# Mixture-of-experts macaron layer: the search for the other experts' thresholds in two goes of four experts instead of three goes of two, its sums shared by VectorE transposes, the residual copied inside DRAM, the rows' factors in halves

## The chip, the cores and the metric

The kernel runs on one core of a Trainium2 chip. The metric is the device time of one execution in microseconds (us). Three runs of the kernel before the change took 1978.52, 1975.33 and 1978.26, a median of 1978.26. The core has five engines, each with its own queue of instructions that it works through in order: PE (TensorE, the matrix products, with PEld for its weight loads), DVE (VectorE), ACT (ScalarE), POOL (GpSimd) and SP (which here only starts transfers). Transfers run on 16 DMA engines.

## The reference

The input `x` holds 4 x 2048 = 8192 tokens of 256 numbers. Three updates follow one another, each with a layer norm before it:

```python
x = x + 0.5 * ffn(layernorm(x), router_w, wg, wu, wd)
x = x + attention(layernorm(x), ...)
x = x + 0.5 * ffn(layernorm(x), router_w, wg, wu, wd)
```

`ffn` is a mixture of 8 experts. Each token goes to the two with the largest router probabilities, with weights that sum to one. An expert takes at most `capacity = int(1.25 * 8192 / 8) = 1280` tokens, those with the largest weights; where weights are equal, the earlier token comes first.

```python
order = jnp.lexsort((-fw, fe))                 # by expert, then by falling weight
rank = jnp.arange(N * K) - starts[se]
keep = rank < capacity
...
eo = jnp.einsum('ecf,efd->ecd', silu(g) * u, wd)   # g = disp @ wg, u = disp @ wu, F = 1024
out = zeros.at[st].add(gathered * (sw * keep)[:, None])
```

So for each expert one has to know the weight of the 1280th token (a threshold, and how many of the tokens that equal it still fit). A threshold is a 32-bit number, and finding it is the "search" below.

## The kernel before

The order in time is: the first router and `route()` (to about 92 us), the experts of the first feed-forward layer (to about 890), the attention (to about 1125), `route()` again, the experts of the second layer, and the last scatters.

**Routing.** `first_router` (L1522) loads x, computes mean and variance of every token on VectorE (L1565), and the logits on PE with router weights `wrx`, from which VectorE has taken the mean (L1609); `wrx` is first cleared by POOL (L1598). `choose` (L280) turns logits into weights. Its inner `for_rows` (L372) makes four factors per token and expert that are appended to each token's row, and `write_rows` (L387) sends the rows to DRAM (`rows`), from where the experts gather their tokens.

**The search.** Class `Pair` (L393) finds the thresholds of two experts at once. Each expert's weights lie on 64 partitions, in 4 copies (`COPIES`). A round tests 4 candidates per expert. In the first pair's rounds, counting is on VectorE and all of `route()` waits for it. For the other six experts, `Others` (L524) holds three pairs and gives out their work one step at a time by `others.step()`. In `Pair.steps()` (L427) a round is: ScalarE's `sign` (L432) compares 512 numbers on each partition with that partition's candidate `mark` and sums the signs; PE's `reach` (L436) adds the sums over partitions; VectorE (L437, L440) counts the candidates that are below the threshold and moves `mark`. There are 7 rounds on the upper 16 bits and 7 on the lower ones, then steps that mark (L469 ff., `tail` L491) the tokens above the threshold and equal to it, place them by two scans (L391, L507 to L514), transpose back on PE (L517) and write `slot_lo`: 24 steps for each pair. The first pair takes expert 0 and 1.

**Where the steps stand.** `route()` (L537) takes a step in its rounds 0, 3 and 4 and in every even round from 6, and one in its tail. `first_list` and `first_turn` (L819) take some. In the expert stage, `aside(k)` (L1040) is called at places in the written order of chunk k's work, and takes one step every time until nothing is left.

**The experts.** A layer has 16 chunks of 640 rows, two per expert. `units(k)` (L888) forms the gate and up products by a scheme like Strassen's, in four parts p = 0 to 3, with three PSUM banks in turn (`banks`, L884). In each part, products are named by their number: after the fifth product there is a call to `aside` in the odd chunks, after the fourth one in all chunks for p = 0 to 2; `down(k)` (L1093) forms the down product and calls `aside` once near its end. Within the experts, PE, VectorE and ScalarE work in the order in which the code names the operations, so an operation that waits holds up all that follows it on its engine; POOL's order is a scheduler's. POOL also issues the gathers of rows (L775) and the scatters of results into `dst` (L1048), which adds to what is there.

**The residual.** In the first layer, the results are added to `acc`, a DRAM copy of x. It is written from SBUF (`xw`) by four transfers of 2 MB on SP's queue (L1622), three ahead of the rows, and one behind them. Expert 0's down weights (`wdt`, L720, `load_down`) follow, and expert 1's weights once gather 0 has been issued and has finished (`after`).

**Set-up.** Constants are made in lines 88 to 215, most of them on POOL, whose queue holds them in the order of a scheduler ahead of the clearing of `wrx`.

## Time and profile before

The profile is of one execution that took 1976.69 us.

| what | us |
|---|---|
| three runs, median | 1978.26 (1975.33 to 1978.52) |
| the profiled execution | 1976.69 |
| its span, first to last instruction | 1974.9 |
| PE busy | 1866.0 (94%) |
| VectorE busy | 1372.7 (70%) |
| ScalarE busy | 1030.4 (52%) |
| POOL busy | 1030.3 (52%) |
| first issue of gather 0 in layer 1 | 84.33 |
| first result `y` of layer 1 | 134.9 |
| first scatter into `acc` | 146.1 |

A row of a timeline gives start, duration, engine, line, operation, output and inputs with partitions x elements, and in brackets how long the engine was idle before it and whose end it waited for. In the windows, a row gives the stretch, its length, the busy time and number of instructions of PE, PEld, VectorE, ScalarE and POOL, the mean granted clock of PE (1 is full), and what share of the DMA engines was busy. In the rows of the 40 slices, each digit stands for 49.4 us of the span, in tenths.

### The profile page before, as it was taken

What the parts mean: (1) busy time and instruction counts of PE and PEld (TensorE: products, weight loads), DVE (VectorE), ACT (ScalarE), POOL (GpSimd) and SP (SyncE); (2) the same over time, 40 slices, a digit from 0 to 9 for tenths busy, and PEclk for the clock granted to TensorE, in tenths of its full rate; (3) what the DMA queues carried; (4) which work ended last, traced back from release to release, by engine and by line L of the source; (5) the groups of instructions that cost most, each with busy time, mean ns of one, the idle gap of its engine ahead of it and who ended that gap; (6) DMA issues with size and microseconds to landing.
All of it is one profiled execution on the core that took longest, in us unless ns stands there. A gap on an engine that the chain in (4) does not pass through costs nothing.

```text
span 1974.9 us, 26091 instructions
## 1 busy us (share of the span) xinstructions
PE 1866.0 (94%) x8882; PEld 1338.4 (68%) x8882; DVE 1372.7 (70%) x2677; ACT 1030.4 (52%) x2598; POOL 1030.3 (52%) x1061
## 2 busy tenths in 40 slices
PE   7499999999999999999999659999999999999997
PEld 5366766676667777776888536666666666777776
DVE  8678677776777676646677667867686767676763
ACT  5273747374736463325566437374737473737332
POOL 6434555555555555535555435555545554555552
PEclk9599999999999999999999869999999999999999
DMA  9912232222222221115012541313131313132121
GB/s 346 308 50 75 46 74 47 71 50 71 50 71 50 71 50 28 29 22 178 22 43 90 201 160 18 92 25 96 22 90 26 95 26 88 30 96 28 31 28 19
DMA packets 108005, 148.90 MB, mean 75 GB/s; under 512 B 7512, under 2 KB 94560, under 8 KB 107872
## 3 DMA queue, kind: packets, MB, share of 16 engines
q1 hardware_dynamic: 76992, 103.16, 15.3%
q0 software_dynamic: 30720, 43.93, 13.7%
q8 instruction: 70, 1.15, 0.2%
q14 instruction: 63, 0.52, 0.1%
q10 hardware_dynamic: 160, 0.14, 0.1%
HBM read 91.11 MB, written 56.10 MB: 75 GB/s over the span
## 4 chain that ended last, share of the span: by engine, by line
PE 46%; DVE 4%; ACT 2%; issue 1%; POOL 1%; DMA 1%; POOLq 0%; SPq 0%; DVEq 0%; ACTq 0%
PE mm L899 23%; PE mm L1114 11%; PE py L1412 3%; PE pc L1354 3%; PE qp L1295 3%; DVE ct L840 1%; PE back L1066 1%; PE tr L801 1%; PE trq L1342 1%; DVE junk_a L562 1%; PE trx L1287 1%; DVE key L514 0%; PE ix L699 0%; ACT lo L693 0%; POOL out_dram L1048 0%
## 5 line engine op out<-in xcount | busy, mean ns | idle before, releaser
L899 PE MATMUL mm<-xs,ws 128*128 128x320 f32 x1536 | 479.3, 435 | 1.7 <-DVE u L840 1.7
L843 POOL TENSOR_TENSOR ct<-ct 128x320 f32<-128x320 f32 x360 | 337.0, 936 | 200.9 <-DVE ct L930 151.7
L899 PEld LDWEIGHTS mm<-xs,ws 128*128 128x128 f32 x1536 | 282.2, 190 | 116.8 <-DVE ct L840 6.6
L840 DVE TENSOR_TENSOR ct<-u,mm 128x640 f32<-128x640 f32 x256 | 209.5, 819 | 151.3 <-PE mm L899 110.5
L775 POOL DMA_INDIRECT r<-rows,ixs x160 | 156.6, 979 | 273.3 <-ACT eo L1047 197.1
L927 ACT ACTIVATE ct<-ct 128x960 f32<-128x960 f32 (+1 forms) x192 | 141.2, 735 | 299.2 <-DVE ct L840 285.9
L840 DVE TENSOR_TENSOR ct<-ct,mm 128x640 f32<-128x640 f32 x288 | 236.0, 819 | 72.9 <-PE mm L899 57.2
L1114 PE MATMUL mm<-ct,wds 128*128 128x320 f32 x960 | 279.6, 433 | 1.0 <-DVE ct L840 1.0
L693 ACT ACTIVATE lo<-from_below,behind_lo 128x129 f16<-128x129 f16 x896 | 272.8, 395 | 0.0
L1114 PEld LDWEIGHTS mm<-ct,wds 128*128 128x128 f32 x960 | 178.7, 190 | 75.0 <-DVE ct L840 7.0
L1114 PE MATMUL mm<-ct,wdt 128*128 128x320 f32 x720 | 217.2, 438 | 0.0
L1048 POOL DMA_INDIRECT acc<-eo,ixs x80 | 128.0, 1600 | 146.4 <-ACT eo L1047 128.4
L1048 POOL DMA_INDIRECT out_dram<-eo,ixs x80 | 127.9, 1599 | 146.3 <-ACT eo L1047 128.4
L899 PE MATMUL mm<-xsT,wgt 128*128 128x320 f32 x512 | 189.9, 453 | 3.0 <-ACT p L939 2.0
L899 PE MATMUL mm<-xsT,wut 128*128 128x320 f32 x512 | 179.6, 432 | 0.0
L930 DVE TENSOR_TENSOR ct<-ct 128x640 f32<-128x640 f32 (+1 forms) x128 | 158.1, 1235 | 22.0 <-ACT ct L927 22.0
L1114 PEld LDWEIGHTS mm<-ct,wdt 128*128 128x128 f32 x720 | 133.4, 193 | 49.3 <-issue 4.2
L840 DVE TENSOR_TENSOR u<-p,mm 128x640 f32<-128x640 f32 x126 | 103.4, 821 | 87.6 <-PE mm L899 56.1
L899 PE MATMUL mm<-xsT,ws 128*128 128x320 f32 x512 | 161.8, 439 | 2.4 <-DVE ct L840 2.4
L939 ACT COPY p<-mm 128x640 f32<-128x640 f32 x126 | 86.4, 686 | 90.1 <-PE mm L899 74.5
L899 PEld LDWEIGHTS mm<-xsT,ws 128*128 128x128 f32 x512 | 97.4, 191 | 43.9 <-DVE ct L840 4.3
L899 PEld LDWEIGHTS mm<-xsT,wut 128*128 128x128 f32 x512 | 97.3, 190 | 40.6 <-issue 0.2
(340 smaller groups left out, 2932.9 us busy)
## 6 DMA issues: line engine op xcount, KB each, us to landing
wgt<-in_L_ffn_wg_dram SPq DMA_DIRECT2D x16, 1024.0 KB
wut<-in_L_ffn_wu_dram SPq DMA_DIRECT2D x16, 1024.0 KB
wdt<-in_L_ffn_wd_dram SPq DMA_DIRECT2D x16, 1024.0 KB
rows<-xw SPq DMA_DIRECT2D x6, 2240.0 KB
xw<-in_L_attn_x_dram SPq DMA_DIRECT2D x16, 512.0 KB
acc<-xw SPq DMA_DIRECT2D x4, 2048.0 KB
out_dram<-xw SPq DMA_DIRECT2D x16, 512.0 KB
xw<-acc SPq DMA_DIRECT2D x15, 512.0 KB
```

The source lines that it names most:

```text
L693: nc.scalar.activation(lo[:, t, :], from_below, AF.Sign, bias=at, scale=1.0)
L775: gathers[k].append(nc.gpsimd.indirect_dma_start(out=r, out_offset=None, in_=src[:, :], in_offset=bass.IndirectOffsetOnAxis(ap=lists[e][:, ...
L840: nc.vector.tensor_tensor(o, a, b, op)
L843: nc.gpsimd.tensor_tensor(o, a, b, op)
L899: nc.tensor.matmul(ps, a, b, start=start, stop=True, skip_group_check=not start)
L927: nc.scalar.activation(h(p)[:, qs, :], h(p)[:, qs, :], AF.Silu)
L930: engine.tensor_tensor(h(p)[:, qs, :], h(p)[:, qs, :], hT(p)[:, qs, :], ALU.mult)
L939: nc.scalar.copy(p1, ps)
L1048: ins = nc.gpsimd.indirect_dma_start(out=dst[:, :], out_offset=bass.IndirectOffsetOnAxis(ap=lists[e][:, i0 + i : i0 + i + 1], axis=0), in_ ...
L1114: nc.tensor.matmul(ps, a(p), b(p), start=(p == 0 and not more), stop=(p == NF - 1), skip_group_check=more)
L1295: nc.tensor.matmul(qp[i][:, k, 0:W1], xT[i][:, k, c, :], wqx[:, c, :], start=(c == 0), stop=(c == DC - 1))
L1354: nc.tensor.matmul(pcs[b][:, c, 0 : D + 1], eks[i][:, k, c * P : (c + 1) * P], ring[i % 4][:, k, :], start=(first and k == 0), stop=(last ...
```

## The change

1. The other six experts are searched by class `Quad` in two goes of four experts with 32 partitions each and 2 copies. The first takes experts 2 to 5, the second experts 4 to 7, of which it keeps 6 and 7. With 2 candidates instead of 4, there are 9 + 11 rounds instead of 7 + 7, and 28 steps to a go. `marked`, `placed` and `back` work on 256 columns instead of 128, and what was two steps is one (`placed`).
2. In the expert stage (`far`), the sums over partitions of a round are made on VectorE: a transpose of 32 x 32 blocks of the sums into 32 columns of `shift` (read as half floats) and a reduction into two columns of `rstd`. In `route()`, two PE products do it.
3. The steps have places and due times: `step_at` takes a step only if the place's time (49 us for each chunk, plus the place's own) has reached the time when the last step was taken plus its stated length (7.5 us for a round, 3.2 in chunk 1). The fifth product is followed by a place in all chunks, and for p = 3 too.
4. `route()` takes steps in odd rounds from 5 (five instead of four) and two in its tail instead of one; `first_turn` takes four instead of three.
5. `acc` is filled by four transfers from x to `acc` inside DRAM, behind gather 0 and ahead of expert 1's weights on SP. Expert 0's down weights are loaded with its others.
6. In the first routing, the rows' factors are made in two halves of the tokens; the copy `raw` comes between them.
7. The set-up constants change accordingly (a ladder for 2 copies, `quad_of`, `quad_ahead`, `portions`, `flip`, `quads`), and some are gone.

```diff
-    minus_half_of = const.tile([P, P], F16, name="minus_half_of")
-    nc.gpsimd.tensor_scalar(minus_half_of, half_of, -1.0, None, ALU.mult)
     half_ahead = const.tile([P, P], F16, name="half_ahead")
     nc.gpsimd.tensor_tensor(half_ahead, half_of, before, ALU.mult)
-    minus_half_ahead = const.tile([P, P], F16, name="minus_half_ahead")
-    nc.gpsimd.tensor_scalar(minus_half_ahead, half_ahead, -1.0, None, ALU.mult)
-    half_cap = const.tile([P, 1], F16, name="half_cap")
-    nc.gpsimd.memset(half_cap, CAP / float(SEG))
-    half_nowhere = const.tile([P, 1], F16, name="half_nowhere")
-    nc.gpsimd.memset(half_nowhere, (-1.0 - NOWHERE) / SEG)
+    QUAD = 4
+    quad_of = blocks(P // QUAD, "quad_of", setup)
+    quad_ahead = const.tile([P, P], F16, name="quad_ahead")
+    nc.gpsimd.tensor_tensor(quad_ahead, quad_of, before, ALU.mult)
+
+    portions = const.tile([P, 4], F16, name="portions")
+
+    def shares(parts, k):
+        nc.gpsimd.memset(portions[:, k : k + 1], -CAP * parts / float(P))
+        nc.gpsimd.memset(portions[:, k + 1 : k + 2], (-1.0 - NOWHERE) * parts / P)
+        return portions[:, k : k + 1], portions[:, k + 1 : k + 2]
+
+    half_shares, quad_shares = shares(PAIR, 0), shares(QUAD, 2)
...
+    def ranks_of(groups, copies, name):
+        ranks = setup.tile([P, MARKS], F32, name=f"ranks_{name}")
+        nc.gpsimd.iota(
+            ranks, pattern=[[0, groups], [1, copies]], base=1, channel_multiplier=0, allow_small_or_imprecise_dtypes=True
+        )
+        nc.vector.tensor_tensor(ranks, heads[:, :: P // MARKS], ranks, ALU.mult)
+        which = setup.tile([P, 1], F32, name=f"which_{name}")
+        nc.vector.tensor_reduce(which, ranks, AX.X, ALU.add)
+        return which
+
+    def ladder(copies, rounds, cols, which, name):
+        rungs = const.tile([P, sum(rounds), cols], F32, name=f"rungs_{name}")
+        moves = const.tile([P, sum(rounds) + len(rounds)], F32, name=f"moves_{name}")
+        firsts = []
+        for unit, many in zip(UNITS, rounds):
+            at = sum(rounds[: len(firsts)])
+            strides = [unit * (copies + 1) ** (many - 1 - n) for n in range(many)] + [0.0]
+            for n in range(many):
+                nc.gpsimd.memset(rungs[:, at + n, :], strides[n])
+                nc.gpsimd.memset(moves[:, at + n : at + n + 1], strides[n + 1] - strides[n])
+            nc.gpsimd.memset(moves[:, sum(rounds) + len(firsts) :], strides[0])
+            firsts.append(moves[:, sum(rounds) + len(firsts) : sum(rounds) + len(firsts) + 1])
+        nc.gpsimd.tensor_tensor(moves, moves, which.to_broadcast([P, sum(rounds) + len(rounds)]), ALU.mult)
+        return rungs, moves, firsts
+
+    ROUNDS_B = (9, 11)
+    COPIES_B = MARKS // QUAD
+    which_b = ranks_of(QUAD, COPIES_B, "b")
+    rungs_a, moves_a, firsts_a = ladder(COPIES, (ROUNDS, ROUNDS), MARKS + 1, ranks_of(PAIR, COPIES, "a"), "a")
+    rungs_b, moves_b, firsts_b = ladder(COPIES_B, ROUNDS_B, COPIES_B, which_b, "b")
+    for first, unit in zip(firsts_b, UNITS):
+        nc.gpsimd.tensor_scalar(first, first, -0.5 * unit, None, ALU.add)
+    nc.gpsimd.tensor_scalar(which_b, which_b, -1.0, None, ALU.add)
+    quads = [const.tile([P, P], F16, name=f"quad_{g}") for g in range(COPIES_B)]
+    nc.gpsimd.tensor_scalar(quads[1], quad_of, which_b, None, ALU.mult)
+    nc.gpsimd.tensor_tensor(quads[0], quad_of, quads[1], ALU.subtract)
...
+    across = shift.bitcast(F16)[:, :32]
...
+        pieces = [slice(k, k + n // 2) for k in (0, n // 2)] if n == T else [slice(0, n)]
+
+        def wide(x, some):
+            return spread(x[:, some].unsqueeze(2), [P, some.stop - some.start, E])
+
+        def for_rows(some):
             if n == T:
-                nc.scalar.activation(factor, by_token, AF.Sign)
-                nc.scalar.mul(halves, by_token, 0.5)
+                nc.scalar.activation(factor[:, some], by_token[:, some], AF.Sign)
+                nc.scalar.mul(halves[:, some], by_token[:, some], 0.5)
             else:
                 nc.gpsimd.tensor_scalar(halves, by_token, 0.5, None, ALU.mult)
                 nc.gpsimd.tensor_scalar(factor, by_token, 0.0, None, ALU.is_gt)
-            nc.gpsimd.tensor_tensor(by, factor, tok(shift[:, ts]), ALU.mult)
-            nc.gpsimd.tensor_tensor(factor, factor, tok(rstd[:, ts]), ALU.mult)
-
+            nc.gpsimd.tensor_tensor(by[:, some], factor[:, some], wide(shift[:, ts], some), ALU.mult)
+            nc.gpsimd.tensor_tensor(factor[:, some], factor[:, some], wide(rstd[:, ts], some), ALU.mult)
+
+        for some in pieces:
+            ins = nc.gpsimd.tensor_tensor(by_token[:, some], p0[:, some], wide(rs, some), ALU.mult)
+            after(ins, (last,), "the first pair's weights come first")
         if n < T:
-            for_rows()
+            for_rows(pieces[0])
         else:
-            yield for_rows
+            for some in pieces:
+                yield partial(for_rows, some)
...
-            def turn(half, n):
-                reach = self.bank("reach")[:, : MARKS + 1]
-                nc.tensor.matmul(reach, s["part"].to_broadcast([P, P]), own_b, start=True, stop=True)
-                nc.vector.scalar_tensor_tensor(
-                    s["seen"], reach, MOST_ABOVE, rungs_b[:, half, n, :], ALU.is_le, ALU.mult, accum_out=s["ahead"]
-                )
-                nc.vector.tensor_scalar(mark, s["ahead"], mark, None, ALU.add)
...
+        def marked(self, wt, n):
+
+            self.cand = self.s["cand"].bitcast(F32)
+            self.tie, self.above, self.place = self.junk[:, :n], self.junk[:, n : 2 * n], self.key[:, :n]
+            parts = self.s["parts"]
...
+        def placed(self, same, ahead, shares):
+
+            tie, above, place, parts, nums = self.tie, self.above, self.place, self.s["parts"], self.s["nums"]
+            cap, nowhere = shares
...
+        def reached(self):
+            part = self.s["part"]
+            if not self.alone:
+                reach = self.bank("reach")[:, :COPIES_B]
+                for g in range(COPIES_B):
+                    nc.tensor.matmul(reach[:, g : g + 1], quads[g], part, start=True, stop=True)
+                return reach
+            reach = rstd[:, :COPIES_B]
+            nc.vector.transpose(across, part.to_broadcast([P, 32]))
+            nc.vector.tensor_reduce(reach, across.rearrange("p (g k) -> p g k", g=COPIES_B), AX.X, ALU.add)
+            return reach
+
+        def sign(self, key):
+            s = self.s
+            with nc.allow_low_precision(reason="sums of at most 512 signs are exact in half floats"):
+                nc.scalar.activation(self.junk, key, AF.Sign, bias=s["mark"], scale=-1.0, accum_out=s["part"])
+            self.alone = self.far
+
+        def turn(self, n):
+            s, mark = self.s, self.s["mark"]
+            nc.vector.scalar_tensor_tensor(
+                s["seen"][:, :COPIES_B], self.reached(), MOST_ABOVE, rungs_b[:, n, :], ALU.is_le, ALU.mult,
+                accum_out=s["ahead"],
+            )
+            nc.vector.tensor_scalar(mark, s["ahead"], mark, moves_b[:, n : n + 1], ALU.add, ALU.add)
+
+        def rounds(self, key, half):
+            first = sum(ROUNDS_B[:half])
+            self.sign(key)
+            yield 0
+            for n in range(first, first + ROUNDS_B[half] - 1):
+                self.turn(n)
+                self.sign(key)
+                yield 0
+            self.turn(first + ROUNDS_B[half] - 1)
+
+        def steps(self):
...
+            yield from self.rounds(self.key, 1)
+            nc.vector.tensor_scalar(s["cand"], mark, 0.5 * UNITS[1], float(1 << 16), ALU.add, ALU.mult)
+            nc.vector.tensor_tensor(s["cand"], s["cand"], s["top"], ALU.bitwise_or)
+            yield 3
...
+            self.placed(quads, quad_ahead, quad_shares)
+            yield 7
+            es = slice(self.e + self.take.start, self.e + self.take.stop)
+            back = self.back().rearrange("p (j e t) -> p e t j", j=2, e=QUAD)[:, self.take]
...
+            rest = (key2, scratch, smalls_b)
+            self.searches = [Quad(PAIR, slice(0, QUAD), *rest), Quad(E - QUAD, slice(PAIR, QUAD), *rest)]
+            self.left = chain.from_iterable(search.steps() for search in self.searches)
...
+        def step_at(self, at, pace):
+            if at >= self.due:
+                self.due = at + (self.step() or pace)
...
-                if at > 4 and at % 2 == 0:
+                if at > 4 and at % 2:
                     others.step()
...
-            if n == 2:
-                others.step()
+            others.step()
...
             for _ in range(3):
                 others.step()
                 stay_busy(spare, 1)
+            others.step()
...
-                if k % PER:
-                    aside(k)
+                aside(k, "fifth", p)
...
-                    aside(k)
+                    aside(k, "fourth", p)
...
+        PLACES = {"fifth": (7.3, 15.2, 23.2, 31.0), "fourth": (10.6, 18.6, 26.6), "end": (45.8,)}
+
+        def aside(k, place, p=0):
+
+            others.step_at(k * 49.0 + PLACES[place][p], 3.2 if k == PER - 1 else 7.5)
...
-            aside(k)
+            aside(k, "end")
...
+                for b in range(B):
+                    some = slice(b * N, (b + 1) * N)
+                    after(nc.sync.dma_start(out=acc[some, :], in_=x_rows[some, :]), gathers[0], "the first rows come first")
                 load_expert(1, wpool, weights, gathers[0])
             first_turn()
+            others.start()
...
-            load_expert(0, wpool, weights, whole=False)
+            load_expert(0, wpool, weights)
...
-                nc.gpsimd.tensor_copy(raw, w[:, PAIR:, :])
-                for more in for_rows:
+                for n, more in enumerate(for_rows):
                     more()
-                batches = [slice(b * NJ, (b + 1) * NJ) for b in range(B)]
-                for n, b in enumerate(batches[: B - 1] + batches + batches[B - 1 :]):
-                    if B - 1 <= n < 2 * B - 1:
-                        write_rows(xw, rows[0], b)
-                    else:
-                        nc.sync.dma_start(out=acc_tiles[:, b, :], in_=xw[:, b, 0:D])
-                load_down(0, weights)
+                    if n == 0:
+                        nc.gpsimd.tensor_copy(raw, w[:, PAIR:, :])
+                for b in range(B):
+                    write_rows(xw, rows[0], slice(b * NJ, (b + 1) * NJ))
```

## The prediction

> **What bounds the kernel now.** I read the page's first, second and fourth parts, then the windows of the second expert stage, two timelines inside it, and the start.
>
> Busy time and the 40 slices, first:
>
> ```profile
> PE 1866.0 (94%) x8882; PEld 1338.4 (68%) x8882; DVE 1372.7 (70%) x2677; ACT 1030.4 (52%) x2598; POOL 1030.3 (52%) x1061
> ...
> PE   7499999999999999999999659999999999999997
> PEclk9599999999999999999999869999999999999999
> ```
>
> TensorE is the bound, except in slices 1 and 2 (the first routing, 49 to 98 us) and around slice 23 (attention and the second routing). So a step of the search beside the experts costs only what it makes PE wait or execute. The windows show how much; they are pairs of chunks in the second expert stage:
>
> ```profile
> 1205.52:1306.34 100.82, 98.91 (x459) 68.81 (x458) 74.16 (x124) 56.81 (x147) 53.66 (x47) 1.00 0.26 59
> 1306.34:1405.75 99.41, 98.82 (x453) 68.11 (x452) 70.67 (x129) 58.77 (x154) 55.11 (x47) 1.00 0.26 60
> 1405.75:1508.24 102.49, 100.58 (x458) 69.83 (x458) 73.71 (x124) 56.94 (x147) 52.72 (x47) 0.98 0.26 59
> 1508.24:1607.67 99.43, 98.83 (x452) 68.13 (x452) 70.69 (x129) 58.76 (x154) 55.07 (x47) 1.00 0.26 60
> 1607.67:1709.42 101.75, 99.85 (x454) 69.47 (x454) 73.63 (x123) 54.37 (x141) 52.61 (x47) 0.98 0.26 59
> 1709.42:1806.09 96.67, 96.67 (x443) 68.27 (x442) 67.18 (x95) 51.75 (x134) 54.19 (x47) 1.00 0.27 62
> 1806.09:1902.57 96.48, 96.48 (x443) 68.34 (x442) 67.28 (x95) 43.33 (x104) 53.98 (x47) 1.00 0.18 29
> ```
>
> First column after the stretch: length; then PE, PEld, DVE, ACT, POOL. The last two pairs have no search; their mean is 96.58. The five others exceed it by 503.90 - 482.90 = 21.0 us. A pair with rounds alone costs 2.8 (ten turns), a pair with the marking, placing and transposing back 4.2 to 5.9. With an estimated 1.1 for chunk 0, which lies outside, the search costs this layer about 22.1. From first to last result of a stage (`y`) layer 1 takes 1.5 less (695.6 against 697.1): 20.6.
>
> Next, one round as it is, VectorE and ScalarE in the second of these stretches:
>
> ```profile
> 1338.22 0.16 DVE L437 SCALAR_TENSOR_TENSOR seen_b<-reach,rungs_b 128x9 f32<-128x9 f32 x1
> 1338.30 0.08 DVE L437 DVE_READ_ACCUMULATOR seen_b<-reach,rungs_b 128x1 f32 x1
> 1338.49 0.21 DVE L440 TENSOR_SCALAR mark_b<-ahead_b,mark_b 128x1 f32<-128x1 f32 x1
> 1338.62 1.48 DVE L930 TENSOR_TENSOR ct<-ct 128x1280 f32<-128x1280 f32 x1
> ```
>
> ```profile
> 1338.80 0.72 ACT L432 ACTIVATE scratch<-upper,mark_b 128x512 f16<-128x512 int16 x1 [2.63 <-DVE seen_b L437]
> 1339.43 0.19 ACT L432 ACTIVATION_READ_ACCUMULATOR scratch<-upper,mark_b 128x1 f16 x1
> 1339.52 0.67 ACT L939 COPY p<-mm 128x640 f32<-128x640 f32 x1
> ```
>
> The turn takes VectorE 0.40 us and the sign starts 0.58 after the turn does. The copy `p` waits behind the sign on ScalarE, and ends at 1340.19; PE's product into the bank that `p` frees starts at 1340.65, 2.43 after the turn (2.29 without the `reach` ahead of it), and loads its weights some 0.27 earlier. There is little left.
>
> Last, the start. VectorE:
>
> ```profile
> 6.28 0.24 DVE L1609 TENSOR_TENSOR wrx<-wrT,wr_mean 128x16 f32<-128x16 f32 x1 [1.53 <-POOL wrx L1598]
> 6.44 5.31 DVE L1565 BATCH_NORM_STATS2 st<-xw 128x6 f32<-128x256 f32 x16
> ```
>
> It idles 1.53 us for POOL's clearing of `wrx` (6.10), and from then on is busy 9.86 and 9.77 of 10 us in the windows 10 to 20 and 20 to 30, up to the statistics' end at 30.7, on which the routing chain stands.
>
> **The search in the chunks, per layer.** It goes from three searches of 24 steps to two of 28 (20 rounds instead of 14 each); 12 of 72 steps lay outside the chunks, now 15 of 56 (routing, first turn). What remains by the due times: 15 turns in a "fifth" place with p up to 2, five there with p = 3, about nine in "fourth" and "end", and the copies, `marked`, `placed` and `back` twice.
>
> A turn there no longer has `reach` on PE (0.11 us each; 0.17 shown, overlapped). Instead VectorE transposes 128x32 halves and reduces 128x32 to 128x2. Neither is in the trace. Rows near: the cast 128x16 0.17, reduce 128x8<-128x64 0.22, 128x16<-128x128 0.28; bounds 0.2 (both at the smallest spacing of chained small operations, about 0.1) to 0.6 together. I take 0.18 + 0.18 + 0.04 hand-over each = 0.44: nearest to the cast and the smaller reduce. The mark comes 0.44 later, the `p` copy ends 2.41 after the turn's start instead of 1.97, and PE wants it at about 2.02 (load) to 2.29 (product): a stall of about 0.27, bounds 0.1 and 0.45. 15 x 0.27 = 4.1 (1.5 to 6.8). Queued behind it are L930 and L840 on VectorE, which have the same 0.44 to give.
>
> At p = 3 PE goes on into the down product with a shorter lead. In the chunk before that has top/key/mark there (1354.24 to 1355.30, 1.06 us of VectorE) PE lost 0.62 before L1114. I take 0.7 for odd chunks (k3, k5), 1.1 for turn plus `cand` (k6) and 1.9 where the sign also stands before the silu and the list's L693 on ScalarE (k0, k4): 6.3; bounds 0.4 each (2.0) and about 2.2 each (11).
>
> Turns in "fourth" and "end": no near wait; 1.2 (0 to 4).
>
> `placed` in k1 at p = 3: the two scans, copies and products now on 256 columns in one step, about 3.1 us of VectorE; before, halves of it were split over two steps. I take 4.3 with what it meets on POOL, then 0.75 for `marked` and `back` there, copies in k2 0.7, `high`/top in k4 0.3, k6 and k7 1.1: 7.1 (4 to 10). The row for what it meets:
>
> ```profile
> 1251.18 2.79 DVE L514 SCALAR_TENSOR_TENSOR key<-key,nums_b,scratch 128x128 f32<-128x128 f32 x1
> ```
> ```profile
> 1250.83 3.00 POOL L930 TENSOR_TENSOR ct<-ct 128x1280 f32<-128x1280 f32 x1
> ```
>
> The same form takes 0.35 us in both routings, where POOL is idle. It ends with POOL's operation.
>
> Sum per layer 4.1 + 6.3 + 1.2 + 7.1 = 18.7 against 20.6 and 22.1: **-1.9 and -3.4**, -5.3 together. The bounds are 7.5 and 31.8.
>
> [...] Before, the turn's `seen` read PSUM and SBUF; now both inputs (`rstd`, `rungs_b`) lie in SBUF. [...]
>
> **The start.** POOL's set-up queue. `wrx`'s clearing is now behind two more selects (0.26 each), `half`, `half_ahead`, `quad_ahead` (0.52, 0.42, 0.42), four `less_a` (0.98) and some 30 more memsets of 0.037 net: adding the queue up from the rows of before gives 11.05 instead of 6.10, **+4.95**. VectorE's statistics stand behind it in order. Only if the loads of x were the pace would it vanish: 8.4 MB at the 344 to 358 GB/s of these windows is 24 us, as long as VectorE's, but they run on while VectorE waits. Bounds 0 and +5.5. Late next: PE's first logits (8.29, now about 11.4), and all of the routing.
>
> Factors of rows in halves and no `acc` ahead of the rows on SP: the rows can go about 2 us sooner after the routing weights (before, three `acc` writes held the queue to 54.1). They were not the last for gather 0; nothing by itself.
>
> Gather 0's neighbours: in layer 1 its issue stands at 84.33, the first normalised row at 92.05, the first result at 134.9; the same chain in layer 2, shifted by 1078.94, gives 83.13, 86.1 and 130.56. In layer 1 the DMA share is 0.95 to 1.06 in 54 to 105 (`rows`, the last `acc`, `wdt` still queued), and VectorE waits 7.95 for the row. After, `wdt` goes with the first weights, and the DRAM copies stand behind gather 0: **-4.3**, bounds 0 and -5.6.
>
> The DRAM copies: 8.4 MB from about 91, 25 us at 345 GB/s, 49 at half of that (read and written in DRAM). The first scatter into `acc` is at 146.1, so nothing is seen; the cover is gone above 55 us, and then POOL's gathers stand behind the scatter (up to +10). Expert 1's weights behind them on SP are wanted about 90 us later.
>
> **Routing.** Five turns beside it instead of four, two steps in the tail instead of one. A loop round is 1.26 us without and 1.57 with a turn: +0.31; tail +0.34; **+1.3** for both layers (0 to 2). The merged placing there takes one step less, which only shortens the yields.
>
> **Sum.** -5.3 + 4.95 - 4.3 + 1.3 = -3.4. The profiled execution took 1976.69 (span 1974.9), 1.57 below the median 1978.26: 1973.3, and against the median **1974.9**. Plus or minus 0.2% (4 us) is what a measurement of this kernel can tell from none.
>
> **The rivals.**
> *Slack swallows the turns.* The p = 3 turns at 0.4 and the others at 0.11: 1.5 + 2.0 + 1.2 + 7.1 = 11.8 a layer, 13.8 less in all: 1961. For it: PE waits little in a pair with ten turns. Against: `p` ends 0.05 to 0.3 before it is wanted.
> *The turn's chain on VectorE and its lock with POOL, slower.* Place: "fifth", p = 3, and the sign behind it. With 0.45 for 15 and twice the price at p = 3: 6.8 + 12.6 + 1.2 + 7.1 = 27.7 a layer, 18 more in all: 1993. The change is zero at 20.4 us a layer, and slower beyond the bound from 22.4.
> *The set-up's delay is hidden*: 1970.
> *The DRAM copy is late at the first scatter*: 1985.
>
> **How the numbers follow.** Forecast 0.38 (its own range 1970 to 1981), slack 0.24, lock 0.28, hidden set-up 0.05, late copy 0.05. Faster: 0.17 of the forecast's, slack, set-up: 0.46. Same: 0.21. Slower: 0.28 + 0.05 = 0.33. The range 1960 to 1994 leaves out about a tenth on each side (half of slack's cases, a third of lock's).
>
> **What would show it.** VectorE's first statistics at about 11.4 (set-up). The first row 3 us after gather 0's issue (neighbours). Pairs of chunks: 96.6 from k8 on, and about 18 us of excess before; stalls of PE on `p` in "fifth" places about 0.3; a `seen_b` of more than 0.5 us would be the lock. First scatter: POOL waiting for the DMA of `acc` would be the late copy. Wrong altogether if the pairs without search change.

## The result, and the profile after

The changed kernel takes **1986.75 us** (median of 6 runs, 1985.04 to 1991.22), the kernel before 1978.05 beside it (6 runs, 1975.33 to 1978.52): a ratio of **1.0050**, 95% interval 1.0037 to 1.0063. It is slower by 0.5%, some 9 us.

The profiled execution took 1986.13. The head of its page, and the line of busy times:

```profile
span 1984.3 us, 26077 instructions
PE 1863.4 (94%) x8838; PEld 1332.7 (67%) x8838; DVE 1382.5 (70%) x2741; ACT 1025.5 (52%) x2582; POOL 1034.6 (52%) x1100
```

PE is busy 2.6 us less than before, VectorE 9.8 us more, and the span is 9.4 us longer: PE waits longer. The costliest groups (busy time, mean, then idle time just before them and who ended it) show two of these waits. Before, the first stood at 1.0 us of idle time and the second at 3.0:

```profile
L1181 PE MATMUL mm<-ct,wds 128*128 128x320 f32 x960 | 284.9, 439 | 11.6 <-DVE ct L906 11.4
L965 PE MATMUL mm<-xsT,wgt 128*128 128x320 f32 x512 | 187.4, 448 | 9.4 <-ACT p L1005 7.0
```

The windows of the second layer, pairs of chunks at the same places of the work as in the prediction (stretch, length, then busy times of PE, PEld, VectorE, ScalarE and POOL, granted clock, DMA share, GB/s):

```profile
1216.69:1321.64 104.95, 99.78 (x453) 68.22 (x452) 78.06 (x146) 59.28 (x153) 52.88 (x46) 0.98 0.25 57
1321.64:1423.82 102.18, 100.61 (x449) 68.57 (x448) 74.55 (x144) 58.23 (x152) 56.41 (x49) 1.00 0.25 58
1423.82:1524.96 101.14, 98.81 (x438) 66.44 (x437) 73.49 (x146) 58.93 (x154) 54.01 (x47) 1.00 0.26 59
1524.96:1622.17 97.21, 97.21 (x453) 68.31 (x452) 70.70 (x109) 51.30 (x132) 52.74 (x45) 1.00 0.27 61
1622.17:1718.85 96.68, 96.68 (x443) 68.29 (x442) 67.17 (x95) 51.80 (x134) 54.20 (x47) 1.00 0.27 62
```

The pairs without search keep their length (96.68, against 96.67 before), so the experts' own work is untouched. The search now ends earlier, in chunk 7; but the first pair, 8.3 us above 96.68, is dearer than any was before (5.9 at most), and the next two, with 5.5 and 4.5, are among the dear ones there (2.8 to 5.9).

Followed through the timelines of the two profiled executions, the 9.4 us come from here ("cast" is VectorE's first operation on the finished first list, `u` the first of chunk 0's, `y` the first result of a chunk):

| stretch | before | after | difference | predicted |
|---|---|---|---|---|
| first statistics on VectorE | 6.44 | 11.28 | +4.84 | +4.95 |
| from there to the first cast (at 81.27 and at 87.29) | 74.83 | 76.01 | +1.2 | +0.65 |
| cast to `u`, layer 1 (gather 0 and its neighbours) | 20.29 | 16.42 | -3.9 | -4.3 |
| `u` to the first `y`, layer 1 (chunk 0) | 33.33 | 36.81 | +3.5 | in the next row |
| first `y` of chunk 0 to first `y` of chunk 14, layer 1 | 695.61 | 696.28 | +0.7 | -1.9 with chunk 0 |
| from there to the cast of layer 2 | 329.72 | 331.75 | +2.0 | +0.65 |
| cast to `u`, layer 2 | 15.99 | 16.13 | +0.1 | 0 |
| `u` to the first `y`, layer 2 (chunk 0) | 33.34 | 36.03 | +2.7 | in the next row |
| first `y` of chunk 0 to first `y` of chunk 14, layer 2 | 697.05 | 695.31 | -1.7 | -3.4 with chunk 0 |

The forecast by these rows was -3.4 and +9.4 came, an error of 12.8 us. Eight tenths of it are in the chunks: -5.3 was forecast and +5.1 came. Chunk 0 of the two layers alone grew by 6.2 us, and the other chunks together saved 1.1.

### The profile page after: what moved, and what is told of

It is laid out like the page before. It is cut to its first block, busy times and chain, and to the rows that moved or that the text cites. A ratio compares the mean times of both kernels' runs of the same rounds, so it can differ in the third digit from the quotient of the medians.

```text
span 1984.3 us, 26077 instructions
## 1 busy us (share of the span) xinstructions
PE 1863.4 (94%) x8838; PEld 1332.7 (67%) x8838; DVE 1382.5 (70%) x2741; ACT 1025.5 (52%) x2582; POOL 1034.6 (52%) x1100
## 4 chain that ended last, share of the span: by engine, by line
PE 43%; DVE 6%; ACT 3%; issue 1%; POOL 1%; DMA 1%; POOLq 0%; DVEq 0%; SPq 0%; ACTq 0%
PE mm L965 22%; PE mm L1181 9%; PE py L1483 3%; PE pc L1425 3%; PE qp L1366 3%; DVE ct L906 1%; PE back L1133 1%; ACT lo L762 1%; PE tr L866 1%; PE trq L1413 1%; PE trx L1358 1%; DVE junk_a L632 1%; DVE ws L818 0%; ACT r L855 0%; PE ix L768 0%
## 5 line engine op out<-in xcount | busy, mean ns | idle before, releaser
L1181 PE MATMUL mm<-ct,wds 128*128 128x320 f32 x960 | 284.9, 439 | 11.6 <-DVE ct L906 11.4
L762 ACT ACTIVATE lo<-from_below,behind_lo 128x129 f16<-128x129 f16 x896 | 272.9, 396 | 0.0
L996 DVE TENSOR_TENSOR ct<-ct 128x640 f32<-128x640 f32 (+1 forms) x128 | 158.0, 1235 | 25.1 <-ACT ct L993 25.1
L965 PEld LDWEIGHTS mm<-xsT,wgt 128*128 128x128 f32 x512 | 88.2, 189 | 65.2 <-ACT p L1005 36.1
```

The costliest lines, as they stand in the source:

```text
L762: nc.scalar.activation(lo[:, t, :], from_below, AF.Sign, bias=at, scale=1.0)
L965: nc.tensor.matmul(ps, a, b, start=start, stop=True, skip_group_check=not start)
L996: engine.tensor_tensor(h(p)[:, qs, :], h(p)[:, qs, :], hT(p)[:, qs, :], ALU.mult)
L1181: nc.tensor.matmul(ps, a(p), b(p), start=(p == 0 and not more), stop=(p == NF - 1), skip_group_check=more)
```

## The experiments

All ratios below are to the kernel before, run beside each on the same chip. Four kernels shared a chip in each of three groups. The best kernel was in two groups, and its ratio came out as 0.9938 and 0.9967; so differences of less than 0.3% between groups say little, and places in the traces carry the finer points. The changed kernel itself ran in none of the three groups. acc_from_sbuf, which differs from it in the residual alone, stands beside wrx_first and pe_sums on the same chip, and there they are 0.30% and 0.64% better. A trace is one execution as well: from gather 0 to `u` in layer 1 the best kernel took 12.3 us in one and 14.6 in the other.

| kernel | median us | ratio to before | 95% interval |
|---|---|---|---|
| the changed kernel | 1986.75 | 1.0050 | 1.0037 to 1.0063 |
| wrx_first | 1981.26 | 1.0021 | 1.0012 to 1.0030 |
| acc_from_sbuf | 1989.17 | 1.0051 | 1.0037 to 1.0065 |
| before_dram | 1977.28 | 0.9996 | 0.9987 to 1.0005 |
| pe_sums | 1974.80 | 0.9987 | 0.9978 to 0.9996 |
| dead_transposes | 1973.21 | 1.0000 | 0.9991 to 1.0009 |
| both_mended | 1961.44 | 0.9938 | 0.9924 to 0.9951 |
| both_sbuf | 1963.72 | 0.9960 | 0.9947 to 0.9974 |
| both_split | 1964.36 | 0.9961 | 0.9947 to 0.9974 |
| mended_again (both_mended) | 1972.32 | 0.9967 | 0.9955 to 0.9980 |
| mended_rows_whole | 1970.96 | 0.9959 | 0.9947 to 0.9972 |
| mended_no_f2 | 1972.25 | 0.9970 | 0.9958 to 0.9982 |
| mended_three | 1970.90 | 0.9967 | 0.9956 to 0.9978 |

(The kernel before had a median of 1976.56 beside the four from wrx_first to pe_sums, 1972.79 beside the four from dead_transposes to both_split, and 1976.60 beside the last four.)

### The set-up queue on POOL: wrx_first

```diff
     row_of_ones = ones[:, :1].to_broadcast([P, BANK])
+    wrx = const.tile([P, DC, 32], F32, name="wrx")
+    nc.gpsimd.memset(wrx, 0.0)
...
-    wrx = const.tile([P, DC, 32], F32, name="wrx")
...
             with tc.manual_schedule(engines=ENGINES):
-                nc.gpsimd.memset(wrx, 0.0)
```

> The changed kernel with the clearing of wrx put ahead of the other set-up constants on POOL, all else the same. Theory (the set-up queue delays the whole first stage): the first statistics start at about 6.3 us instead of 11.28, gather 0 is issued at about 84.4 instead of 89.3, and the time falls by 4 to 5 us, to about 1982. Rival (the loads of x pace that stage, or the ladders that POOL makes after it are then late): no change, 1986.7.

In the changed kernel VectorE waits 3.69 us for POOL's set-up (the bracket names the instruction of POOL that was last by the profile, one behind `wrx`'s clearing at 11.00):

```profile
11.18 0.17 DVE L1680 TENSOR_TENSOR wrx<-wrT,wr_mean 128x16 f32<-128x16 f32 x1 [3.69 <-POOL moves_b L205]
11.28 1.07 DVE L1636 BATCH_NORM_STATS2 st<-xw 128x6 f32<-128x256 f32 x3
```

With the clearing first:

```profile
4.55 0.23 DVE L1680 TENSOR_TENSOR wrx<-wrT,wr_mean 128x16 f32<-128x16 f32 x1
4.70 1.39 DVE L1637 BATCH_NORM_STATS2 st<-xw 128x6 f32<-128x256 f32 x4
```

The statistics start 6.6 us earlier, gather 0 is issued at 84.89 instead of 89.30, and the ratio falls from 1.0050 to 1.0021, some 5.7 us, though between two chips. The theory holds: the trace alone has 4.4 us. The other 2.2 of the 6.6 us are lost between the statistics and gather 0.

### The residual: acc_from_sbuf and before_dram

acc_from_sbuf undoes this part in the changed kernel; before_dram makes it alone in the kernel before.

```diff
-                for b in range(B):
-                    some = slice(b * N, (b + 1) * N)
-                    after(nc.sync.dma_start(out=acc[some, :], in_=x_rows[some, :]), gathers[0], "the first rows come first")
...
-                for b in range(B):
-                    write_rows(xw, rows[0], slice(b * NJ, (b + 1) * NJ))
+                batches = [slice(b * NJ, (b + 1) * NJ) for b in range(B)]
+                for n, b in enumerate(batches[: B - 1] + batches + batches[B - 1 :]):
+                    if B - 1 <= n < 2 * B - 1:
+                        write_rows(xw, rows[0], b)
+                    else:
+                        nc.sync.dma_start(out=acc_tiles[:, b, :], in_=xw[:, b, 0:D])
+                load_down(0, weights)
```

> The changed kernel with the residual written from SBUF as before (three transfers ahead of the rows, one behind them, then expert 0's down weights). Theory (the transfers beside gather 0 cost the first layer 3.9 us): the first normalised row comes about 8 us after gather 0's issue instead of 4.5, and the time rises by 3 to 5 us, to about 1990.5. Rival (copies inside DRAM contend with the gathers as much): the same time, 1986.7, or less.

> The kernel before with only one part of the change: the residual copied inside DRAM behind gather 0, expert 0's down weights loaded with its others. Theory: the first normalised row comes 2 to 5 us after gather 0's issue, and the time falls by about 4 us, to 1974. Rival (the gain belongs to the new search's timing): the same as before, 1978.

Neither theory fits well. By the ratios, undoing it costs nothing measurable (1.0051 against 1.0050), and made alone it gains 0.04% with an interval from -0.13% to +0.05%, so at most 2.6 us. The traces show that the first row comes sooner: with the copies inside DRAM the first row is normalised 3.1 us after gather 0's issue in before_dram, and 7.7 after it before; in acc_from_sbuf 6.5, in the changed kernel 4.5. Of these 4.6 us in before_dram, 3.0 are left at `u`, counted from gather 0's issue (14.2 instead of 17.2 us; 14.4 and 17.3 in the other pair). The five tiles' gathers are issued one after the other by POOL, 1.25 to 1.56 us apart, so the fifth stands 5.3 us behind the first. So the forecast -4.3 is about right for the traces up to that place; what of it is left in the time is 0 to 2.6 us in the kernel before. A third pair, below, gives more.

### The sums of a round: pe_sums and dead_transposes

pe_sums keeps PE's two products for `reach` in the expert stage too:

```diff
             for search in self.searches:
-                search.far = True
+                search.far = False
```

> The changed kernel with the sums of a round made by two PE products in the expert stage too, no transposes on VectorE. Theory (the transposes cost little, what costs is where ScalarE's sign stands): a turn is 0.45 us shorter on VectorE, but PE has about 29 x 0.15 us more to do in a layer; both layers together between -4 and +4 us, 1983 to 1991. Rival (the longer turn on VectorE is what made the change slower): 8 us or more faster, 1979 or less.

The ratio is 0.9987 instead of 1.0050: some 12 us, and the kernel is now a little faster than before. The rival holds, and my theory (that the transposes cost little) falls. Chunk 0 and chunks 1 to 14 are 1.9 + 5.3 us shorter in layer 1 and 1.2 + 4.6 in layer 2.

But there are two ways in which a longer turn can cost: VectorE is busy longer, or the mark comes later. dead_transposes tells them apart. It has PE's sums, and after the new mark a transpose and a reduction that nobody reads:

```diff
             nc.vector.tensor_scalar(mark, s["ahead"], mark, moves_b[:, n : n + 1], ALU.add, ALU.add)
+            if self.idle:
+                nc.vector.transpose(across, s["part"].to_broadcast([P, 32]))
+                nc.vector.tensor_reduce(
+                    rstd[:, :COPIES_B], across.rearrange("p (g k) -> p g k", g=COPIES_B), AX.X, ALU.add
+                )
...
-                search.far = True
+                search.idle = True
```

> The kernel with the sums on PE in the expert stage (1974.8), and after each turn's new mark one transpose and one reduction more on VectorE, whose results nobody uses: VectorE works as long as in the changed kernel, but the mark is as early as with PE's sums. Theory (the changed kernel loses its 12 us because the mark, and so the sign and the copy p behind it on ScalarE, come 0.44 us later): 1975 to 1979. Rival (VectorE's time itself is what PE waits for): 1984 to 1988, like the changed kernel.

The same turn (after the fifth product, p = 1, chunk 5 of layer 2) in the three kernels. The changed kernel, VectorE and then ScalarE:

```profile
1455.00 0.20 DVE L510 STREAM_TRANSPOSE shift<-part_b 128x32 f16<-128x32 f16 x1
1455.24 0.18 DVE L511 TENSOR_REDUCE rstd<-shift 128x2 f32<-128x32 f16 x1
1455.46 0.16 DVE L522 SCALAR_TENSOR_TENSOR seen_b<-rstd,rungs_b 128x2 f32<-128x2 f32 x1
1455.55 0.08 DVE L522 DVE_READ_ACCUMULATOR seen_b<-rstd,rungs_b 128x1 f32 x1
1455.67 0.27 DVE L526 TENSOR_SCALAR mark_b<-ahead_b,mark_b,moves_b 128x1 f32<-128x1 f32 x1
```

```profile
1456.03 0.72 ACT L517 ACTIVATE scratch<-key,mark_b 128x512 f16<-128x512 f32 x1 [3.20 <-DVE mark_b L526]
1456.66 0.19 ACT L517 ACTIVATION_READ_ACCUMULATOR scratch<-key,mark_b 128x1 f16 x1
1456.75 0.67 ACT L1005 COPY p<-mm 128x640 f32<-128x640 f32 x1
```

pe_sums, VectorE and then ScalarE's sign:

```profile
1447.04 0.15 DVE L522 SCALAR_TENSOR_TENSOR seen_b<-reach,rungs_b 128x2 f32<-128x2 f32 x1
1447.11 0.08 DVE L522 DVE_READ_ACCUMULATOR seen_b<-reach,rungs_b 128x1 f32 x1
1447.23 0.27 DVE L526 TENSOR_SCALAR mark_b<-ahead_b,mark_b,moves_b 128x1 f32<-128x1 f32 x1
```

```profile
1447.62 0.72 ACT L517 ACTIVATE scratch<-key,mark_b 128x512 f16<-128x512 f32 x1 [3.02 <-DVE seen_b L522]
```

dead_transposes, VectorE:

```profile
1444.98 0.15 DVE L522 SCALAR_TENSOR_TENSOR seen_b<-reach,rungs_b 128x2 f32<-128x2 f32 x1
1445.18 0.27 DVE L526 TENSOR_SCALAR mark_b<-ahead_b,mark_b,moves_b 128x1 f32<-128x1 f32 x1
1445.37 0.20 DVE L528 STREAM_TRANSPOSE shift<-part_b 128x32 f16<-128x32 f16 x1
1445.61 0.18 DVE L529 TENSOR_REDUCE rstd<-shift 128x2 f32<-128x32 f16 x1
```

From the turn's start to the sign's are 1.03 us in the changed kernel, and 0.58 with PE's sums; the transpose takes 0.20 and the reduction 0.18, started 0.24 and 0.22 before what follows. The copy `p` stands behind the sign. How much later VectorE's next operation that waits for PE is than in a chunk without search, step by step through a chunk, gives each place its price:

| place (layer 2) | changed kernel | pe_sums | dead_transposes |
|---|---|---|---|
| fifth, p = 0, 1, 2, chunk 5 | 0.29, 0.32, 0.33 | 0.14, 0.13, 0.14 | 0.14, 0.13, 0.14 |
| fifth, p = 0, 1, chunk 6 | 0.29, 0.32 | 0.14, 0.14 | 0.14, 0.14 |
| fifth, p = 2, chunk 6 | 1.11 | 0.82 | 0.93 |
| chunks 2 to 7 together, above chunks without search | 11.9 | 7.0 | 8.4 |

So with p up to 2 in an odd chunk the whole difference is the mark's lateness: VectorE does the same work in dead_transposes, at no cost. Over chunks 2 to 7, 3.5 of the 4.9 us are lateness and 1.4 the time on VectorE (2.9 and 2.0 in layer 1). The ratio of 1.0000 (theory: 1975 to 1979 us on the chip of pe_sums, that is 0.999 to 1.001) says the same, within what two chips differ. How it divides in the time of the whole kernel is less sure: both_mended below, on the same chip, has neither the unused transposes nor the late set-up and is 0.62% faster, of which wrx_first explains 0.29%.

In the even chunks, the place at p = 2 is dear in all three. ScalarE of the changed kernel in chunk 6, and PE:

```profile
1510.05 2.08 ACT L855 ACTIVATE r<-r 128x256 f32<-128x256 f32 x4
1512.03 2.44 ACT L762 ACTIVATE lo<-from_below,behind_lo 128x129 f16<-128x129 f16 x8
1514.38 0.71 ACT L517 ACTIVATE scratch<-key,mark_b 128x512 f16<-128x512 f32 x1
...
1515.08 0.68 ACT L1005 COPY p<-mm 128x640 f32<-128x640 f32 x1
```

```profile
1515.81 0.81 PE L965 MATMUL mm<-xsT,wgt 128*128 128x320 f32 x2 [1.02 <-ACT p L1005]
```

There the sign has 4.5 us of row scaling (L855) and list making (L762) ahead of it. It starts when they are done, 1.1 us after the new mark, and its 0.9 us go to the copy `p` and on to PE, which idles 1.02 us (0.62 in pe_sums). In the kernel before, the even chunks had no step in a fifth place.

### Both mended, and the residual again: both_mended and both_sbuf

both_mended is wrx_first and pe_sums in one; both_sbuf is that with acc_from_sbuf's edit.

> The changed kernel with the sums on PE in the expert stage and wrx cleared first. Theory (the two causes lie in different stages and add up): 12 + 5 us less than the changed kernel, 1969 to 1971. Rival (the one hides part of the other): 1973 or more.

> The kernel of both_mended with the residual written from SBUF as before. Theory (transfers beside gather 0 cost the first layer 3.9 us, as the profiles of the kernel before and the changed one have it): 3 to 5 us more than both_mended. Rival (that difference is within what one execution differs from another): within 1.5 us of both_mended.

The two gains of 0.29% and 0.63% make 0.9958 if they add up; 0.9938 and, on another chip, 0.9967 were measured. The sum lies between the two, so they add up as far as these chips can tell. This version beats both kernels: it is 0.3 to 0.6% faster than the kernel before, 0.8 to 1.1% faster than the changed one.

both_sbuf is 0.22% slower than both_mended by the ratios, with intervals that just overlap; in the traces the two are alike at `u` (98.39 and 98.36), though gather 0 was issued 1.4 us earlier in both_sbuf. With the two pairs above, the residual's part is worth between nothing and 4 us, and I can't say it better.

### Placing in two steps: both_split

```diff
             need_t, off = (nums[:, k : k + 1] for k in range(2))
             scan(place, tie)
+            yield 3
...
-            yield 4.4
+            yield 3
-            self.placed(quads, quad_ahead, quad_shares)
+            yield from self.placed(quads, quad_ahead, quad_shares)
...
             others.step()
+            others.step()
```

> The kernel of both_mended with the placing in two steps, the first scan apart from what follows; one step more is taken in the first turn, so that the first search still ends in chunk 1. Theory (the placing at p = 3 in one step holds PE for 4.3 us at once, which is followed by 3.4 us at half the clock): chunk 1 is 2 to 4 us shorter in each layer, 1962 to 1967. Rival (the scans and copies cost the same in two pieces): 1969 to 1971.

The placing step in the changed kernel at the end of chunk 1's units, PE's products behind it, and the window that follows:

```profile
1270.98 4.88 PE L1181 MATMUL mm<-ct,wds 128*128 128x320 f32 x12 [4.29 <-DVE ct L906]
```

```profile
1272.00:1276.00 4.00, 4.00 (x14) 2.62 (x13) 3.33 (x7) 0.84 (x2) 0.00 (x0) 0.77 0.00 0
```

PE waits 4.29 us at once, and afterwards the clock is granted at 0.77 in that window: twelve products take 4.88 us instead of 3.47. With two steps:

```profile
1256.49 3.47 PE L1185 MATMUL mm<-ct,wds 128*128 128x320 f32 x12 [2.91 <-DVE ct L910]
```

2.91 us, and the full clock. Chunk 1 is 2.2 and 3.7 us shorter (54.40 and 52.79, against 56.63 and 56.51 in both_mended), as the theory has it. Yet the time is not shorter: 0.9961 against 0.9938. In the traces the first `u` came 2.2 us later in layer 1 and 2.8 in layer 2, and this takes back most of it. In layer 1 that is the step that was moved into the first turn: gather 0 was issued 0.6 us earlier, but its first row waits for one more turn, and comes 5.8 us after the issue instead of 4.4, and a stretch at half the clock (3.4 us from 91.38) follows, which both_mended does not have. In layer 2 only 0.9 us can be the step's, since gather 0 itself was issued 1.9 us later; most of that, 1.6, comes from a stretch at half the clock in the attention (3.4 us from 941.30), which both_mended does not have there. By these two profiles alone both_split would be 1.3 us faster; why its median is 2.9 us longer stays open.

### The first turn, the rows, and the place at p = 2

> The kernel of both_mended once more, as the reference of the three beside it: 0.992 to 0.995 of the kernel before.

It is the kernel of both_mended on another chip: 0.9967.

mended_three has three steps in the first turn, as before the change:

```diff
-                if at > 4 and at % 2:
+                if at > 4 and (at % 2 or at == 8):
...
                 stay_busy(spare, 1)
-            others.step()
```

> The kernel of both_mended with three steps in the first turn as before, and the fourth taken in round 8 of the routing instead. Theory (the fourth step's sum on PE stands behind the filler products and holds the first row on VectorE for 1 to 1.5 us in the first layer): the first row about 3 us after gather 0's issue instead of 4.4, against 0.35 us more routing in each layer: 0 to 1.5 us faster. Rival (the fifth tile's gather is what the first products wait for): 0.5 to 1 us slower.

In the changed kernel, VectorE at the fourth step and the first row behind it, and POOL's first and fifth gather:

```profile
93.37 0.16 DVE L522 SCALAR_TENSOR_TENSOR seen_b<-reach,rungs_b 128x2 f32<-128x2 f32 x1 [3.12 <-PE reach L507]
...
93.83 0.93 DVE L853 TENSOR_SCALAR r<-r 128x256 f32<-128x256 f32 x2
```

```profile
89.30 1.26 POOL L840 DMA_INDIRECT r<-rows,ixs  x1 [20.80 <-DVE mark_b L526]
...
94.64 0.94 POOL L840 DMA_INDIRECT r<-rows,ixs  x1 [0.30 <-issue]
```

The fourth turn waits for its sums until 93.14, since they stand on PE behind the filler products of `stay_busy`, and the row waits behind the turn. With three steps (gather 0 issued at 84.99):

```profile
86.34 0.16 DVE L523 SCALAR_TENSOR_TENSOR seen_b<-reach,rungs_b 128x2 f32<-128x2 f32 x1 [1.19 <-PE reach L508]
...
88.02 0.41 DVE L854 TENSOR_SCALAR r<-r 128x256 f32<-128x256 f32 x1 [1.12 <-DMA r<-rows,ixs]
```

The row comes 3.0 us after the issue instead of 4.3 (mended_again), as expected. At the fifth row nothing is left of it: in both, VectorE waits for that row's gather and starts on it 8.1 us after the issue. So the last tile's gather decides, as the rival had it. At `u` it is 14.5 and 14.6 us. The ratio is the same, 0.9967.

mended_rows_whole makes the factors in one piece:

```diff
-        pieces = [slice(k, k + n // 2) for k in (0, n // 2)] if n == T else [slice(0, n)]
+        pieces = [slice(0, n)]
```

> The kernel of both_mended with the rows' factors made in one piece. Theory (the rows are not what gather 0 waits for): the same, within 1 us. Rival (the first search waits for POOL and ScalarE to be done with the factors): 1 to 3 us slower.

0.9959 against 0.9967: no difference. The rows are sent 1.7 us later (54.99 instead of 53.28), and nothing waits for them, as forecast.

mended_no_f2 leaves the dear place out:

```diff
         def aside(k, place, p=0):
 
+            if place == "fifth" and p == 2 and k > 0 and k % PER == 0:
+                return
```

> The kernel of both_mended without the fifth place at p = 2 in chunks 2, 4 and 6; its step goes to the fourth place behind it. Theory (there ScalarE has 4.5 us of row scaling and list making ahead of the sign, so that p is late and PE idles 0.6 to 0.7 us): 1 to 3 us faster. Rival (the steps that are put off cost as much where they go): the same within 1 us.

0.9970, no gain. Chunks 4 and 6 are 1.8 and 1.0 us shorter, and PE idles there not at all; but chunks 5 and 7 are 0.5 and 2.3 longer. In chunk 7 the second search's placing now falls on the fifth place at p = 1 instead of p = 0, where more of VectorE's work stands behind it, and PE waits 1.71 us. The rival holds: what one place saves, the next one pays.

## Why the prediction was wrong

The forecast was 1974.9, no change or slightly faster, and 1986.75 came. The step that failed is the search's cost in the chunks, 18.7 us a layer, from which -5.3 followed. The runs show 24.3 and 22.6 in its place, and +5.1. Here are the prediction's terms set on the chunks (the 1.2 for "fourth" and "end" spread over its nine turns, the 1.1 for k6 and k7 halved) beside what each chunk took above a chunk without search; for chunk 0, the growth is added to the 1.1 that was estimated before:

| part of the search | forecast | layer 1 | layer 2 |
|---|---|---|---|
| chunk 0 | 2.8 | 4.6 | 3.8 |
| chunk 1 (`marked`, `placed`, `back`) | 5.1 | 7.6 | 6.9 |
| chunk 2 (copies) | 0.7 | 1.4 | 1.4 |
| chunks 3 to 6 | 9.4 | 10.3 | 10.0 |
| chunk 7 | 0.7 | 0.5 | 0.5 |

Step by step:

- **Set-up, +4.95.** Right: +4.84 in the trace, and 4.4 us at gather 0 when it was undone.
- **The turn on VectorE, 0.44 longer, 0.27 at p up to 2.** Right in size: 0.45 longer, 0.29 to 0.33. So the transposes are not what the forecast missed. But the prediction did not set beside this stall what the same search would cost with PE's sums, 0.13 to 0.14 for a turn and some 12 us less in all. That difference was paid inside the sum and never stood in it as a term of its own, and it is what makes the change slower than the kernel before.
- **"At p = 3 ... 1.9 where the sign also stands before the silu and the list's L693 on ScalarE", in the even chunks.** The place was wrong. The list's work on ScalarE hits the sign at p = 2, where I took the 0.27 of all; it measured 0.9 to 1.1. At p = 3 PE lost about 1.1 us in chunk 4 and 0.65 in chunk 6 where 1.9 and 1.1 were forecast, so that the sum of chunks 3 to 6 is only 0.6 to 0.9 too low.
- **Chunk 0.** Forecast 2.8 against an estimated 1.1 before, so +1.7; the two layers measured +3.5 and +2.7. It is an even chunk, with the dear place in it, and the 1.1 was an estimate without a row. With PE's sums it is 1.9 and 1.2 us shorter; which step in it costs the rest was not traced.
- **`placed` at p = 3, 4.3.** Right: PE waits 4.29 us. What follows it, half the clock for 3.4 us, was not in the sum: about 1.7 us in each layer, most of what chunk 1 is too low by. In mended_no_f2, in layer 2, no such stretch follows, and chunk 1 is 1.7 us shorter than with PE's sums alone (54.27 against 55.96).
- **Copies in chunk 2, 0.7.** Too low: 1.4 in both layers, with VectorE's sums and with PE's.
- **The search before, 20.6 and 22.1.** Nearly right: by the chunks 20.2 and 21.6, with the same 1.1 for chunk 0. Two of the five windows that were shown had a granted clock of 0.98, and the prediction put their price down to the search's work. It is 3.4 us at half the clock in each, some 1.7 us of time, once in layer 1 and twice in layer 2 (before_dram has as many behind the same step, transposing back, two of them in other chunks). The new search has one such stretch in each layer, behind the placing.
- **Neighbours of gather 0, -4.3.** Right in the two profiles (-3.9); by the rows the first result of layer 2 is at 130.61, not 130.56, which changes nothing. No more than 0 to 4 us of it is in the time by three pairs of kernels. The fifth gather's issue, 5.3 us behind the first, is a cover that I did not name.
- **Routing, +1.3.** Too low: +1.2 and +2.0. The five rounds with a turn take 1.65 us instead of the 1.57 taken, and the tail, with two steps, is 0.7 longer in each layer instead of 0.34.
- **The DRAM copies, hidden.** Right: the first scatter is at 151.1, five us later like all else there.
- **Rows in halves, nothing.** Right.

Of the rivals, the late DRAM copy (1985) came nearest in number, by luck, since the copies were not late. The slower turn (1993) had more of what happened: the turn's chain on VectorE and the sign behind it cost time, though its price of 0.45 a turn and twice the forecast at p = 3 was too high. Its second half, the lock with POOL (`seen` held until a POOL product beside it ends), is there but small. The `seen` of a turn at p = 3 in the changed kernel, and POOL at that time:

```profile
1369.84 0.45 DVE L522 SCALAR_TENSOR_TENSOR seen_b<-rstd,rungs_b 128x2 f32<-128x2 f32 x1
```

```profile
1367.36 2.91 POOL L996 TENSOR_TENSOR ct<-ct 128x1280 f32<-128x1280 f32 x1
1370.35 4.80 POOL L909 TENSOR_TENSOR ct<-ct 128x320 f32<-128x320 f32 x4
```

It takes 0.45 instead of 0.16, and ends 0.02 us after L996 does. Of the 80 turns of the changed kernel 12 take 0.38 to 0.54 us (one in each of the chunks 0 and 2 to 6), and each of these ends 0.01 to 0.02 us after a POOL product that ran beside it; of the 80 turns of pe_sums, whose `seen` reads one input from PSUM, none does. So the lock costs 0.2 to 0.4 us once a chunk. L996 beside it takes 2.91 us here, but `seen` begins 0.43 us before that ends.

## What to carry to other kernels

An operation moved from the bounding engine to an idle one is not paid for by its time there, but by who waits behind its result (here, in chunk 5, 0.29 to 0.33 us a turn against 0.13 to 0.14, and 0.13 to 0.14 too where VectorE does the same work after the mark): price the old and the new way of the same step side by side, down to the copy that frees the next PSUM bank. Before a step goes into a place, read the in-order queue of every engine that it touches at that place; here ScalarE had 4.5 us of other work ahead of the sign in every second chunk. And take stalls that the clock turns into lost time (here 3.4 us at half the clock, some 1.7 us each) out of an average before it is called a price.

## What the runs showed of the hardware

- **Short stalls of PE and the clock.** Waits of 1.5 to 1.8 us (transposing back, 2 x 6 cases in the kernel before and before_dram) were followed by 3.4 us at half the clock in 6 of 12 cases. Waits of 3.8 to 4.3 us (placing in chunk 1, 22 cases in 11 kernels) were followed by it in 21, and in 10 of these for 6.8 us. Chunk 1 takes 54.3 us in the one of these cases where the clock stayed full, 55.8 to 56.6 with one such stretch, 56.5 to 57.4 with two. In the traces of the kernel before and of the changed one, all changes of the clock lie 3.413 us or a multiple of it apart. Of the pieces of 3.413 us between these places, 1075 were at full clock with PE busy for at least half of the piece, and none of them was followed by half the clock; 16 were at full clock with PE busy for less, and 15 of them were (in the other one PE was busy for 49%). The six waits behind transposing back in the kernel before are alike, 1.50 to 1.52 us each. In the three that half the clock followed, PE was busy for 1.5 to 1.6 us of the piece ahead of it; in the other three, for 1.7 us or more of every piece that the wait touches.
- **Two products of one column** (`reach` in pe_sums, 128 x 128 by 128 x 1) are so cheap that the whole turn, sign and all, costs 0.13 to 0.14 us where nothing else stands ahead of the sign. The expectation of pe_sums had taken 0.15 for the two products alone.
- **Copies inside DRAM**: 8.4 MB, with gathers and weights, were issued from 97.57 on, and the DMA engines were idle again from about 129 us, some 30 us later; 11.0 MB moved between 84 and 150 us.
